# Layer 3's attention: score tiles on seven single PSUM banks, and six of a block's 32 row sums by accumulating DMA

## The chip, the cores and the metric

The kernel runs on one core of one Trainium2 chip. A core has TensorE (matrix products, written PE in the profile, its weight loads PEld), ScalarE (ACT: exponentials, copies with a scale), VectorE (DVE: elementwise work and reductions), GpSimd (POOL) and SyncE (SP), which run side by side and wait for each other by semaphores, and 16 DMA engines. SBUF is the working memory of 128 partitions. TensorE writes its results to PSUM, which has eight banks of 512 fp32 columns.

The metric is the device time of one execution in microseconds. Before the change it is 2603.03 us, the median of three runs from 2602.6 to 2603.3. The profiled execution has a span of 2601.4 us.

## The reference

The input is four images of 64 x 64 positions with 64 channels in fp32. Four layers run one after the other: a self-attention, a convolution block with layer norms, an attention of the data with itself, and a non-local block. Only the last one, called layer 3, is touched:

```python
N = H * W                                   # 4096 positions
g_x = (x @ g_W + g_b).reshape(B, N, 32)
phi_x = (x @ phi_W + phi_b).reshape(B, N, 32)
theta_x = (x @ theta_W + theta_b).reshape(B, N, 32)
f = einsum('bnd,bmd->bnm', theta_x, phi_x)
f = softmax(f, axis=-1)
y = einsum('bnm,bmd->bnd', f, g_x)
w_y = y @ w_W + w_b
...                                         # batch norm over all images
return x + w_y
```

For each image it makes a 4096 x 4096 matrix of scores, takes exponentials, multiplies them by `g_x`, and divides each row by its sum of exponentials. There are four images, so some 67 million exponentials in this layer.

## The kernel before, in words

**Order of the work.** One Python loop (`run`) lays out every engine's instructions by hand, as a list of items with work that is due some items later. The instruction streams keep that order. Layers 0 and 1 come first, for all images. Then layer 2 and layer 3 alternate: layer 2 of image 0, layer 2 of image 1, layer 3 of image 0, layer 2 of image 2, layer 3 of image 1, layer 2 of image 3, layer 3 of image 2, layer 3 of image 3. So the layer 3 stages of images 0 and 1 stand alone between layer 2 stages, and those of images 2 and 3 run directly one after the other.

**An item of layer 3.** An image's stage has 64 items, in two blocks (`nb`) of 32 (`mc`). A block is half of the image's rows, 2048 of them, as four groups of 512. An item pairs them with 128 of the 4096 columns. Its parts are:

- `scores(n)`, line 1419: eight small matmuls (32 deep, 64 wide, 512 columns) that fill four PSUM banks, all at once on different parts of the array. In the records each fp32 matmul stands twice, so an item has 16.
- two exponentials, lines 1424 and 1425, of 1024 columns each, from PSUM to a tile `e` of 128 x 2048 in SBUF. There are six such tiles in turn.
- `products(n)`, line 1454, issued two items later: four matmuls of `e` with `gx`, which accumulate over the block into one bank (`st["y"]`).
- the sum of exponentials over the columns. Most items add `e` to a running tile `esum` on VectorE (lines 1445 and 1447). Items 9, 19 and 29 of a block, and the last four of the last image, are summed by TensorE instead: four matmuls with a matrix of ones (line 1440) into a second accumulating bank, `st["z"]`.

**End of a block.** `sums` (line 1466) adds the total of `esum` to `st["z"]` by four more matmuls with ones. In the order of TensorE this stands after the scores of the fourth item of what follows, or two items later where layer 2 follows (images 0 and 1). ScalarE copies `st["y"]` out (L1460), takes the reciprocal of the sums as a logarithm and an exponential (L1474, L1477), VectorE refines it by a Newton step (L1482 to L1484), TensorE projects (L1501), ScalarE adds the bias (L1514) and VectorE takes statistics (L1516). In a block that follows directly, the second exponential of item 1 is held back until after the copy of `st["y"]`.

**PSUM.** `PS` is all eight banks. `new_ps` hands out slots of two banks (1024 columns); in layers 2 and 3 three slots take turns, which are banks 0 to 5. `new_acc` alternates between banks 6 and 7, for accumulators. A slot can be written by TensorE again only when ScalarE has read it.

**The `xn` tile.** One tile of 128 x 2048 in SBUF, used in layer 1 alone before the change.

Of the kernel before, what the change touches and what calls it, by code (L numbers as in the profile page):

```python
# [8 lines left out]
F32 = mybir.dt.float32  # L9
AF = mybir.ActivationFunctionType  # L10
ALU = mybir.AluOpType
# [680 lines left out]
def fast_path(ctx: ExitStack, tc: tile.TileContext, a: dict, out: bass.AP, bad):  # L692
    nc = tc.nc
# [10 lines left out]
    xn = ctx.enter_context(tc.tile_pool(name="xn", bufs=1))  # L704
# [4 lines left out]

    PS = pp.tile([128, 4096], F32, name="PS")
    turn_of = {"slots": [0, 1, 2, 3], "ps": 0, "acc": 0}

    def new_ps():
        s = turn_of["slots"][turn_of["ps"] % len(turn_of["slots"])]
        turn_of["ps"] += 1
        return PS[:, bass.ts(s, 1024)]

    def take_slots(*slots):  # L720
        turn_of["slots"], turn_of["ps"] = list(slots), 0

    def new_acc():
        turn_of["acc"] += 1
        return PS[:, bass.ts(6 + turn_of["acc"] % 2, 512)]

# [13 lines left out]
    act = nc.scalar.activation  # L740
# [9 lines left out]
    def fetch_x(b, queues):  # L750
# [17 lines left out]
        out=gam0, in_=a["L0_conv_gamma"].rearrange("(o n) -> o n", o=1).to_broadcast([128, 1])  # L768
# [94 lines left out]
    ones = const.tile([128, 64], F32, name="ones")  # L863
# [422 lines left out]
    def layer2(b):  # L1286
        x, m, first = X[:, b], im[b], len(items)
        xw = x.rearrange("p (w h) -> p w h", h=H)
        m.ph = None
        m.zs = sm.tile([128, 32, 4], F32, tag="zs2", name="zs2")  # L1290
        es, acc = {}, {}
        quads = ((0, 0), (1, 0), (0, 1), (1, 1))

        def scores(n):
            ib = n // 8
            for jb in range(4 * (n % 8), 4 * (n % 8) + 4):
                ps = new_ps()
                for r, c in quads:
                    rows_ = slice(64 * r, 64 * r + 64)
                    mm(  # L1300
                        ps[64 * c : 64 * c + 64, bass.ts(r, 512)],
                        m.ko[rows_, 128 * jb + 64 * c : 128 * jb + 64 * c + 64],
                        m.ko[rows_, bass.ts(2 * ib + r, 512)], start=True, stop=True,
                    )
                if jb % 2 == 0:
                    e = new_e()
                es[n, jb] = e[:, bass.ts(jb % 2, 1024)]
                act(es[n, jb], ps, AF.Exp, bias=SHIFT2, accum_out=m.zs[:, jb, ib : ib + 1])  # L1308
                follow(0)

        def products(n):
            ib = n // 8
            if n % 8 == 0:
                acc[0], acc[1] = new_acc(), new_acc()
            for jb in range(4 * (n % 8), 4 * (n % 8) + 4):
                for r, c in quads:
                    rows_ = slice(64 * r, 64 * r + 64)
                    mm(  # L1318
                        acc[r][64 * c : 64 * c + 64, :], xw[rows_, jb, :],
                        es[n, jb][rows_, bass.ts(c, 512)], start=jb == 0, stop=jb == 31,  # L1320
                    )
            if n % 8 == 7:
                if m.ph is None:
                    m.ph = new_big("ph")
                nc.scalar.copy(m.ph[:, 2048:2560], acc[0])  # L1325
                nc.vector.tensor_add(m.ph[:, 2048:2560], m.ph[:, 2048:2560], acc[1])  # L1326

        def turn(ib):
            ps = new_ps()
            for i in range(4):  # L1330
                nc.tensor.transpose(
                    ps[:, bass.ts(i, 128)], m.ph[:, 2048 + 128 * i : 2176 + 128 * i], ident
                )
# [23 lines left out]


    wys, early = {}, []
    small = {}  # L1360
    held = []

# [44 lines left out]
    def layer3(b):  # L1407
# [3 lines left out]
        def scores(n):  # L1411
            nb, mc = n // 32, n % 32
            e = es[n] = new_e()
            tiles = [new_ps(), new_ps()]
            for kp in range(2):
                for c in range(2):
                    for i in range(2):
                        rows_ = slice(64 * kp + 32 * i, 64 * kp + 32 * i + 32)
                        mm(  # L1419
                            tiles[kp][64 * c : 64 * c + 64, bass.ts(i, 512)],  # L1420
                            m.ph[rows_, 128 * mc + 64 * c : 128 * mc + 64 * c + 64],
                            m.th[rows_, bass.ts(nb, 512)], start=True, stop=True,
                        )
            act(e[:, 0:1024], tiles[0], AF.Exp)  # L1424
            held.append(lambda: act(e[:, 1024:2048], tiles[1], AF.Exp))  # L1425
            if not (mc == 1 and (nb or last)):
                held.pop()()
            for fn in small.get(first + n, []):
                fn()

        def products(n):
            nb, mc = n // 32, n % 32
            e, esum = es[n], m.tg[:, 2048:4096]
            if mc == 0:
                st["y"] = new_acc()
            if mc % 10 == 9 or (last and n >= 60):
                if mc == 9:
                    st["z"] = new_acc()
                for k in range(4):
                    mm(  # L1440
                        st["z"][32 * k : 32 * k + 32, :], ones[:, 0:32], e[:, bass.ts(k, 512)],
                        start=mc == 9, stop=False,
                    )
            elif mc == 1:
                nc.vector.tensor_add(esum, es[n - 1], e)
            elif mc:
                nc.vector.tensor_add(esum, esum, e)  # L1447
            if last and n == 62:
                return
            if last and n == 63:  # L1450
                sums()
            for i in (n - 1, n) if last and n == 63 else (n,):
                for k in range(4):
                    mm(  # L1454
                        st["y"][32 * k : 32 * k + 32, :], m.gx[:, i % 32, :], es[i][:, bass.ts(k, 512)],
                        start=mc == 0, stop=i % 32 == 31,
                    )
            if mc == 31 and not (last and n == 63):
                st["yz"] = new_t("yz")
                nc.scalar.copy(st["yz"][:, 0:512], st["y"])  # L1460
                if held:
                    held.pop()()

        def sums():
            for k in range(4):
                mm(
                    st["z"][32 * k : 32 * k + 32, :], ones[:, 0:32],
                    m.tg[:, 2048 + 512 * k : 2560 + 512 * k], start=False, stop=True,
                )


        def log(cols):
            st["inv"] = st.get("inv") or new_t("inv")
            act(st["inv"][:, cols], st["z"][:, cols], AF.Ln)  # L1474

        def exp(cols):
            act(st["inv"][:, cols], st["inv"][:, cols], AF.Exp, scale=-1.0)  # L1477

        def newton(nb):
            yz, z, t = st["yz"], st["z"], st.pop("inv")  # L1480
            r, d = t[:, 0:512], t[:, 512:1024]
            nc.vector.tensor_mul(d, z, r)  # L1482
            stt(d, d, -2.0, r, ALU.add, ALU.mult, accum_out=inv3[:, 2 * b + nb : 2 * b + nb + 1])
            stt(yz[:, 0:512], d, -1.0, yz[:, 0:512], ALU.mult, ALU.mult)  # L1484

        def totals(n):
            sums()
            steps = [
                lambda: log(slice(0, 256)), lambda: log(slice(256, 512)),
                lambda: exp(slice(0, 256)), lambda: exp(slice(256, 512)), lambda: newton(n // 32),  # L1490
            ]
            for i, fn in enumerate(steps):
                if n == 63 and b < 2:
                    fn()
                else:
                    small.setdefault(first + n + 5 + min(i, 3), []).append(fn)
# [296 lines left out]
```

## Time and profile before

| | us | of the span |
|---|---|---|
| span of the profiled execution | 2601.4 | |
| TensorE busy | 2572.4 | 99% |
| ScalarE busy | 1770.1 | 68% |
| VectorE busy | 1162.7 | 45% |
| GpSimd busy | 14.3 | 1% |
| layer 3, image 0: item 3's scores to item 63's | 134.0 | |
| layer 3, image 1: the same | 134.0 | |
| layer 3, images 2 and 3: item 3's scores to the last item's | 287.1 | |
| VectorE's adds of `e` (L1447), 213 of 2.291 us | 488.0 | |
| exponentials of layer 3 (L1424, L1425), 512 | 524.2 | |
| sums on TensorE (L1440), 216 records | 28.5 | |

Times are microseconds. "Busy" is the time in which an engine executes at least one instruction; TensorE's matmuls are pipelined, several at once on different parts of the array, and their ends are modelled, so that its busy share tells little. The start times are better evidence. A group in the profile is a line of the kernel, an engine and an operation, with the tile written, an arrow, and the tiles read; a busy time and a mean in nanoseconds of one; and after a bar the idle time of the engine before it, with what ended that idle time.

### The profile page before, as it was taken

What the parts mean: (1) busy time and instruction counts of PE and PEld (TensorE: products, weight loads), DVE (VectorE), ACT (ScalarE), POOL (GpSimd) and SP (SyncE); (2) the same over time, 40 slices, a digit from 0 to 9 for tenths busy, and PEclk for the clock granted to TensorE, in tenths of its full rate; (3) what the DMA queues carried; (4) which work ended last, traced back from release to release, by engine and by line L of the source; (5) the groups of instructions that cost most, each with busy time, mean ns of one, the idle gap of its engine ahead of it and who ended that gap; (6) DMA issues with size and microseconds to landing.
All of it is one profiled execution on the core that took longest, in us unless ns stands there. A gap on an engine that the chain in (4) does not pass through costs nothing.

```text
span 2601.4 us, 55343 instructions
## 1 busy us (share of the span) xinstructions
PE 2572.4 (99%) x24477; PEld 870.8 (33%) x24477; DVE 1162.7 (45%) x1302; ACT 1770.1 (68%) x2814; POOL 14.3 (1%) x46
## 2 busy tenths in 40 slices
PE   9999999999999999999999999999999999999998
PEld 3343333333333345333333322233322333322223
DVE  2010266312672237613671168610078500098996
ACT  4666766667666676666656578756588655678886
POOL 2000000000000000000000000000000000000000
PEclk9999999999999999999999999999999999999999
DMA  3000000001000000010010000010000010010002
GB/s 75 1 18 1 17 18 2 17 2 34 1 2 17 17 17 2 1 33 18 1 34 17 18 1 2 2 34 1 18 1 2 4 31 1 1 34 2 1 2 67
DMA packets 24557, 36.75 MB, mean 14 GB/s; under 512 B 3724, under 2 KB 12149, under 8 KB 24309
## 3 DMA queue, kind: packets, MB, share of 16 engines
q1 hardware_dynamic: 22853, 30.72, 5.3%
q8 instruction: 194, 3.18, 0.5%
q10 hardware_dynamic: 752, 1.85, 0.2%
q0 software_dynamic: 704, 0.56, 0.1%
q14 instruction: 54, 0.44, 0.1%
HBM read 4.80 MB, written 4.19 MB: 3 GB/s over the span
## 4 chain that ended last, share of the span: by engine, by line
PE 96%; ACT 2%; DVE 1%; issue 0%; DMA 0%; SPq 0%; ACTq 0%; DVEq 0%
PE PS L1318 17%; PE PS L1300 17%; PE PS L1095 16%; PE PS L1069 16%; PE PS L1419 11%; PE PS L1454 10%; PE PS L1179 2%; PE PS L1440 1%; ACT e L1074 1%; PE PS L1037 1%; PE PS L1241 1%; PE PS L1264 1%; PE PS L1144 1%; PE PS L1398 1%; ACT q L1019 0%; PE PS L952 0%
## 5 line engine op out<-in xcount | busy, mean ns | idle before, releaser
L1074 ACT ACTIVATE e<-PS 128x1024 f32<-128x1024 f32 x512 | 524.1, 1024 | 326.8 <-PE PS L1069 284.2
L1308 ACT ACTIVATE e<-PS 128x1024 f32<-128x1024 f32 x512 | 517.2, 1025 | 292.3 <-PE PS L1300 289.1
L1095 PE MATMUL PS<-e,vq 64*64 64x512 f32 x4096 | 539.9, 591 | 0.0
L1069 PE MATMUL PS<-X,q 64*64 64x512 f32 x4096 | 537.1, 590 | 1.8 <-DVE X L953 1.7
L1447 DVE TENSOR_TENSOR tg<-tg,e 128x2048 f32<-128x2048 f32 x213 | 488.0, 2291 | 23.9 <-ACT e L1425 5.7
L1300 PE MATMUL PS<-ko 64*64 64x512 f32 x4096 | 469.2, 591 | 2.2 <-ACT ko L1282 1.7
L1318 PE MATMUL PS<-e,X 64*64 64x512 f32 x4096 | 464.1, 591 | 0.0
L1424 ACT ACTIVATE e<-PS 128x1024 f32<-128x1024 f32 x256 | 262.8, 1027 | 84.4 <-PE PS L1419 63.6
L1212 DVE SCALAR_TENSOR_TENSOR y<-pad,vec,y 128x1024 f32<-128x1024 f32 x240 | 308.1, 1284 | 8.2 <-ACT pad L1196 1.1
L1419 PE MATMUL PS<-tg,ph 32*64 32x512 f32 x4096 | 311.0, 613 | 0.5 <-ACT e L1424 0.5
L1454 PE MATMUL PS<-e,tg 128*32 128x512 f32 x2048 | 271.8, 603 | 0.0
L1425 ACT ACTIVATE e<-PS 128x1024 f32<-128x1024 f32 x256 | 261.4, 1021 | 0.0
L1069 PEld LDWEIGHTS PS<-X,q 64*64 64x64 f32 x4096 | 161.2, 133 | 279.3 <-issue 231.9
L1300 PEld LDWEIGHTS PS<-ko 64*64 64x64 f32 x4096 | 156.5, 132 | 290.1 <-issue 199.8
L1095 PEld LDWEIGHTS PS<-e,vq 64*64 64x64 f32 x4096 | 160.7, 133 | 272.8 <-issue 171.3
L1318 PEld LDWEIGHTS PS<-e,X 64*64 64x64 f32 x4096 | 155.5, 133 | 275.0 <-issue 271.6
L1082 DVE TENSOR_REDUCE sums<-zs 128x1 f32<-128x4 f32 x128 | 19.9, 155 | 374.3 <-ACT e L1074 374.2
L1326 DVE TENSOR_TENSOR ph<-ph,PS 128x512 f32<-128x512 f32 x16 | 11.0, 687 | 391.7 <-ACT ph L1325 391.7
L1419 PEld LDWEIGHTS PS<-tg,ph 32*64 32x64 f32 x4096 | 80.6, 129 | 217.2 <-issue 119.7
L1454 PEld LDWEIGHTS PS<-e,tg 128*32 128x32 f32 x2048 | 43.6, 108 | 201.0 <-issue 196.9
L1308 ACT ACTIVATION_READ_ACCUMULATOR e<-PS 128x1 f32 x512 | 106.5, 208 | 0.0
L1074 ACT ACTIVATION_READ_ACCUMULATOR e<-PS 128x1 f32 x512 | 99.6, 194 | 0.1
(193 smaller groups left out, 947.5 us busy)
## 6 DMA issues: line engine op xcount, KB each, us to landing
xn<-t SPq DMA_DIRECT2D x64, 128.0 KB
ph<-tg SPq DMA_DIRECT2D x64, 128.0 KB
ko<-ko SPq DMA_DIRECT2D x16, 256.0 KB
xr<-in_x_dram SPq DMA_DIRECT2D x13, 256.0 KB
q<-q SPq DMA_DIRECT2D x12, 256.0 KB
out_dram<-o SPq DMA_DIRECT2D x7, 256.0 KB
out_dram<-o ACTq DMA_DIRECT2D x2, 512.0 KB
out_dram<-o SPq DMA_DIRECT2D x2, 512.0 KB
```

The source lines that it names most:

```text
L1069: mm(ps[64 * c : 64 * c + 64, bass.ts(r, 512)], m.q[rows_, 128 * t + 64 * c : 128 * t + 64 * c + 64], x[rows_, bass.ts(g, 512)], start=Tru ...
L1074: act(es[g // 2][:, bass.ts(g % 2, 1024)], ps, AF.Exp, bias=SHIFT0, accum_out=zs[:, g : g + 1],)
L1095: ins = mm(PS[64 * s : 64 * s + 64, 2048 + 512 * j : 2560 + 512 * j], vq[rows_, :], es[j // 2][rows_, k : k + 512], start=t == 0 and i < 2 ...
L1212: stt(y1, win, wt, y1, ALU.mult, ALU.add)
L1300: mm(ps[64 * c : 64 * c + 64, bass.ts(r, 512)], m.ko[rows_, 128 * jb + 64 * c : 128 * jb + 64 * c + 64], m.ko[rows_, bass.ts(2 * ib + r, 5 ...
L1308: act(es[n, jb], ps, AF.Exp, bias=SHIFT2, accum_out=m.zs[:, jb, ib : ib + 1])
L1318: mm(acc[r][64 * c : 64 * c + 64, :], xw[rows_, jb, :], es[n, jb][rows_, bass.ts(c, 512)], start=jb == 0, stop=jb == 31,)
L1419: mm(tiles[kp][64 * c : 64 * c + 64, bass.ts(i, 512)], m.ph[rows_, 128 * mc + 64 * c : 128 * mc + 64 * c + 64], m.th[rows_, bass.ts(nb, 51 ...
L1424: act(e[:, 0:1024], tiles[0], AF.Exp)
L1425: held.append(lambda: act(e[:, 1024:2048], tiles[1], AF.Exp))
L1447: nc.vector.tensor_add(esum, esum, e)
L1454: mm(st["y"][32 * k : 32 * k + 32, :], m.gx[:, i % 32, :], es[i][:, bass.ts(k, 512)], start=mc == 0, stop=i % 32 == 31,)
```

## The change

It has three parts, all in layer 3.

- **Single banks in turn.** `take_banks(7)` makes `new_bank` hand out banks 0 to 6 one by one. An item takes four, and the next item goes on where it stopped. Bank 7 is `st["y"]` for all blocks. `st["z"]` is no longer an accumulator over the block: `totals` takes one bank from the turn for the closing sums, VectorE copies it into `yz` and so frees it. For the last two items of the last image the turn is restarted on six banks, since bank 6 is then `st["z"]`. Layer 2 goes back to three slots with `take_slots`.
- **First exponential on one bank.** An item's exponentials are one of 512 columns and one of 1536, in place of two of 1024. Where the three banks of the latter wrap from 6 to 0, it is cut in two.
- **Six sums by DMA, none on TensorE.** The `e` tiles of items 3, 7, 11, 15, 19 and 23 of each block go into the `xn` tile by DMA from GpSimd's queue, in two halves of 1024 columns each: the first is a plain copy, the other five accumulate. At item 27 VectorE adds that tile to `esum`. TensorE's sums at items 9, 19 and 29 are gone; those of the last image's last four items stay.

The aim is to let TensorE start an item's scores without waiting for ScalarE, and to take the sums off it without giving VectorE more to do.

```diff
+    def new_bank():
+        if not turn_of["banks"]:
+            turn_of["ps"] += 1
+            return 2 * turn_of["slots"][(turn_of["ps"] - 1) % len(turn_of["slots"])]
+        turn_of["bank"] += 1
+        return (turn_of["bank"] - 1) % turn_of["banks"]
...
+    BY_DMA = (3, 7, 11, 15, 19, 23)
...
-            tiles = [new_ps(), new_ps()]
+            if n == 0 and (b < 3 or not turn_of["banks"]):
+                take_banks(7)
+            if last and n == 62:
+                take_banks(6)
+            banks = [new_bank() for _ in range(4)]
...
-            act(e[:, 0:1024], tiles[0], AF.Exp)
-            held.append(lambda: act(e[:, 1024:2048], tiles[1], AF.Exp))
-            if not (mc == 1 and (nb or last)):
-                held.pop()()
+            def exp(lo, hi):
+                while lo < hi:
+                    k = lo + 1
+                    while k < hi and banks[k] == banks[k - 1] + 1:
+                        k += 1
+                    act(
+                        e[:, 512 * lo : 512 * k],
+                        PS[:, 512 * banks[lo] : 512 * banks[lo] + 512 * (k - lo)], AF.Exp,
+                    )
+                    lo = k
+
+            exp(0, 1)
+            if mc == 1 and (nb or last):
+                held.append(lambda: exp(1, 4))
+            else:
+                exp(1, 4)
+            if mc in BY_DMA:
+                if mc == BY_DMA[0]:
+                    st["dma"] = xn.tile([128, 2048], F32, tag="xn", name="xn")
+                for h in range(2):
+                    cols = bass.ts(h, 1024)
+                    if mc == BY_DMA[0]:
+                        nc.gpsimd.dma_start(out=st["dma"][:, cols], in_=e[:, cols])
+                    else:
+                        nc.gpsimd.dma_start(out=st["dma"][:, cols], in_=e[:, cols], accum_op=ALU.add)
...
-            if mc % 10 == 9 or (last and n >= 60):
-                if mc == 9:
-                    st["z"] = new_acc()
+            st["y"] = PS[:, 3584:4096]
+            if last and n >= 60:
+                st["z"] = PS[:, 3072:3584]
...
-            elif mc:
+            elif mc and mc not in BY_DMA:
                 nc.vector.tensor_add(esum, esum, e)
+            if mc == BY_DMA[-1] + 4:
+                nc.vector.tensor_add(esum, esum, st["dma"])
...
         def totals(n):
-            sums()
+            k = new_bank()
+            z = PS[:, bass.ts(k, 512)]
+            sums(z, True)
+            nc.vector.tensor_copy(st["yz"][:, 512:1024], z)
```

More of the change, by code (lines that the diff above doesn't have):

```diff
@@ L712, in fast_path, with take_banks @@
     PS = pp.tile([128, 4096], F32, name="PS")
-    turn_of = {"slots": [0, 1, 2, 3], "ps": 0, "acc": 0}
-    def new_ps():
+    turn_of = {"slots": [0, 1, 2, 3], "ps": 0, "acc": 0, "banks": 0, "bank": 0}
+    def new_bank():
[4 more added lines that the diff above has]
+        return (turn_of["bank"] - 1) % turn_of["banks"]
+    def take_banks(n):
+        turn_of["banks"], turn_of["bank"] = n, 0
+    def new_ps():
+        if turn_of["banks"]:
+            if turn_of["bank"] % turn_of["banks"] == turn_of["banks"] - 1:
+                turn_of["bank"] += 1
+            k = new_bank(), new_bank()
+            return PS[:, 512 * k[0] : 512 * k[0] + 1024]
         s = turn_of["slots"][turn_of["ps"] % len(turn_of["slots"])]
@@ L720, in take_slots @@
     def take_slots(*slots):
-        turn_of["slots"], turn_of["ps"] = list(slots), 0
+        turn_of["slots"], turn_of["ps"], turn_of["banks"] = list(slots), 0, 0
     def new_acc():
@@ L1295, in scores @@
             ib = n // 8
+            if n == 0 and b:
+                take_slots(0, 1, 2)
             for jb in range(4 * (n % 8), 4 * (n % 8) + 4):
@@ L1417, in scores @@
                     for i in range(2):
-                        rows_ = slice(64 * kp + 32 * i, 64 * kp + 32 * i + 32)
+                        k = 2 * kp + i
                         mm(
-                            tiles[kp][64 * c : 64 * c + 64, bass.ts(i, 512)],
-                            m.ph[rows_, 128 * mc + 64 * c : 128 * mc + 64 * c + 64],
-                            m.th[rows_, bass.ts(nb, 512)], start=True, stop=True,
-                        )
-            act(e[:, 0:1024], tiles[0], AF.Exp)
-            held.append(lambda: act(e[:, 1024:2048], tiles[1], AF.Exp))
-            if not (mc == 1 and (nb or last)):
-                held.pop()()
+                            PS[64 * c : 64 * c + 64, bass.ts(banks[k], 512)],
+                            m.ph[32 * k : 32 * k + 32, 128 * mc + 64 * c : 128 * mc + 64 * c + 64],
+                            m.th[32 * k : 32 * k + 32, bass.ts(nb, 512)], start=True, stop=True,
+                        )
+            def exp(lo, hi):
[22 more added lines that the diff above has]
+                        nc.gpsimd.dma_start(out=st["dma"][:, cols], in_=e[:, cols], accum_op=ALU.add)
             for fn in small.get(first + n, []):
@@ L1433, in products @@
             e, esum = es[n], m.tg[:, 2048:4096]
-            if mc == 0:
-                st["y"] = new_acc()
-            if mc % 10 == 9 or (last and n >= 60):
-                if mc == 9:
-                    st["z"] = new_acc()
+            st["y"] = PS[:, 3584:4096]
+            if last and n >= 60:
+                st["z"] = PS[:, 3072:3584]
                 for k in range(4):
@@ L1441, in products @@
                         st["z"][32 * k : 32 * k + 32, :], ones[:, 0:32], e[:, bass.ts(k, 512)],
-                        start=mc == 9, stop=False,
+                        start=n == 60, stop=False,
                     )
@@ L1450, in products @@
             if last and n == 63:
-                sums()
+                sums(st["z"], False)
             for i in (n - 1, n) if last and n == 63 else (n,):
@@ L1462, in products, with sums @@
                     held.pop()()
-        def sums():
+        def sums(z, alone):
             for k in range(4):
                 mm(
-                    st["z"][32 * k : 32 * k + 32, :], ones[:, 0:32],
-                    m.tg[:, 2048 + 512 * k : 2560 + 512 * k], start=False, stop=True,
+                    z[32 * k : 32 * k + 32, :], ones[:, 0:32],
+                    m.tg[:, 2048 + 512 * k : 2560 + 512 * k], start=alone, stop=True,
                 )
@@ L1473, in log @@
             st["inv"] = st.get("inv") or new_t("inv")
-            act(st["inv"][:, cols], st["z"][:, cols], AF.Ln)
+            act(st["inv"][:, cols], st["yz"][:, 512 + cols.start : 512 + cols.stop], AF.Ln)
         def exp(cols):
@@ L1479, in newton @@
         def newton(nb):
-            yz, z, t = st["yz"], st["z"], st.pop("inv")
+            yz, t = st["yz"], st.pop("inv")
             r, d = t[:, 0:512], t[:, 512:1024]
-            nc.vector.tensor_mul(d, z, r)
+            nc.vector.tensor_mul(d, yz[:, 512:1024], r)
             stt(d, d, -2.0, r, ALU.add, ALU.mult, accum_out=inv3[:, 2 * b + nb : 2 * b + nb + 1])
@@ L1486, in totals @@
         def totals(n):
-            sums()
+            k = new_bank()
+            z = PS[:, bass.ts(k, 512)]
+            sums(z, True)
+            nc.vector.tensor_copy(st["yz"][:, 512:1024], z)
             steps = [
```

## Prediction

> **What bounds the kernel now.** I read the page first, for the engines' shares and the costliest groups, and then only layer 3, since nothing else is changed.
>
> ```profile
> PE 2572.4 (99%) x24477; PEld 870.8 (33%) x24477; DVE 1162.7 (45%) x1302; ACT 1770.1 (68%) x2814; POOL 14.3 (1%) x46
> ...
> L1447 DVE TENSOR_TENSOR tg<-tg,e 128x2048 f32<-128x2048 f32 x213 | 488.0, 2291 | 23.9 <-ACT e L1425 5.7
> ...
> L1424 ACT ACTIVATE e<-PS 128x1024 f32<-128x1024 f32 x256 | 262.8, 1027 | 84.4 <-PE PS L1419 63.6
> L1419 PE MATMUL PS<-tg,ph 32*64 32x512 f32 x4096 | 311.0, 613 | 0.5 <-ACT e L1424 0.5
> ```
>
> The page calls TensorE 99% busy, but its matmuls are pipelined and a group that starts late still counts as busy. So I looked at TensorE's start times inside layer 3, in the timeline (start, length, engine, line).
>
> ```profile
> 1558.63 1.22 PE L1419 MATMUL PS<-tg,ph 32*64 32x512 f32 x16
> 1559.77 1.06 PE L1440 MATMUL PS<-e,ones 128*32 128x512 f32 x8
> 1560.66 1.04 PE L1454 MATMUL PS<-e,tg 128*32 128x512 f32 x8
> 1561.63 1.11 PE L1419 MATMUL PS<-tg,ph 32*64 32x512 f32 x16
> 1562.67 1.06 PE L1454 MATMUL PS<-e,tg 128*32 128x512 f32 x8
> 1563.67 1.28 PE L1419 MATMUL PS<-tg,ph 32*64 32x512 f32 x16
> 1564.88 1.06 PE L1454 MATMUL PS<-e,tg 128*32 128x512 f32 x8
> 1565.87 1.11 PE L1419 MATMUL PS<-tg,ph 32*64 32x512 f32 x16
> ```
>
> An item is scores (L1419) and products (L1454). The one at 1561.63 lasts 1.04 + 1.00 = 2.04 us; the next 1.21 + 0.99 = 2.20. The 0.17 more is scores waiting for a PSUM slot that ScalarE still reads. The sum wave at 1559.77 adds 0.89, of which its neighbour gives back 0.03: 0.86. So an item costs TensorE 2.04 us, waits apart, and a sum on TensorE 0.86.
>
> VectorE is nearly as full there. Its timeline at a block's end, and the stage's windows (span, PE, PEld, DVE, ACT busy):
>
> ```profile
> 1581.73 4.69 DVE L1447 TENSOR_TENSOR tg<-tg,e 128x2048 f32<-128x2048 f32 x2 [0.31 <-ACT e L1425]
> 1592.78 2.29 DVE L1445 TENSOR_TENSOR tg<-e 128x2048 f32<-128x2048 f32 x1 [6.36 <-PE PS L1466]
> 1595.17 7.08 DVE L1447 TENSOR_TENSOR tg<-tg,e 128x2048 f32<-128x2048 f32 x3
> 1603.25 0.69 DVE L1482 TENSOR_TENSOR inv<-PS,inv 128x512 f32<-128x512 f32 x1 [0.99 <-ACT inv L1477]
> ```
> ```profile
> 1519.50:1653.50 134.00, 134.00 (x1500) 30.16 (x1496) 119.48 (x58) 117.72 (x126) 0.00 (x0) 1.00 0.01 1
> ...
> 2276.60:2563.70 287.10, 287.10 (x3192) 67.45 (x3188) 263.95 (x141) 247.05 (x267) 0.00 (x0) 1.00 0.04 9
> ```
>
> From 1592.78 to 1595.17 an add takes 2.39 us with the gap behind it: more than TensorE's 2.04 for the item. VectorE keeps pace now only because TensorE sums every tenth item and items take 2.12 with their waits. The first window runs from item 3's scores to item 63's: 60 items x 2.04 + 7 sum waves x 0.86 + one projection 1.02 = 129.4, so about 4.6 of 134 are waits.
>
> **The skill.** "DMA: Bandwidth & Descriptors", section "SWDGE vs HWDGE vs iDMA": an accumulating DMA can be issued from GpSimd alone, which writes its descriptors. That engine is free: 14.3 us busy in all, at about 0.5 us per DMA issue in its timeline. The same page, "Anatomy of one DMA": some 2 us of fixed cost and then bytes at 436 GB/s. The trace shows less, on copies to 64 partitions: in slices of 0.15 us the copies into ko moved 297 GB/s at best, and a 2.6 us window of the copies into q 202. "Collectives: The Full Stack", section "The bandwidth ceiling": a reducing DMA reads two sources for each write and reached half the rate of a copy. No run here shows an accumulating DMA. "SBUF — State Buffer", section "Who interferes with whom": a VectorE add of two SBUF operands contends with GpSimd's reads, not with descriptor writes. I lean on that; this trace has no GpSimd work beside such adds.
>
> **Sums taken off TensorE.** Line 1440 had three sums in each of seven blocks and six in the last, 27 in all (216 matmul records, 8 each); the new kernel keeps the last block's four. 23 x 0.86 = 19.8 us leave TensorE's path. The closing sums of each block (L1466, 0.86) stay.
>
> **Seven single banks.** Before, an item took two 1024-column slots of three, so the next item's first quad reused the slot of the item before last and its second that of the last item's first exponential. Scores end 1.04 us after they start, the first exponential starts 0.1 later and lasts 1.02: free at 2.17, wanted at 2.04. Hence the waits. Adding L1419's distance to the next group over all 256 items gives 294.0 us, against 256 x 1.044 = 267.3: 26.7 us of waits, some 20 in the steady state. Now only the item's last bank needs the former item's first exponential, of 512 columns. By the 512-column copy (L1325, 587 ns) it ends at 1.15 + 0.59 = 1.74, before 2.04. ScalarE's work barely grows: 1024-column exponentials follow each other at 0.92, that is 0.427 for 512 columns and 0.067 for an instruction. An item needs 4 x 0.427 + 2 x 0.067 = 1.84, and two items in seven, whose last three banks wrap, one instruction more: 1.86 on average. Under 2.04, so hidden, but with only 0.18 to recover from the copy (0.59), logs and exponentials (0.4 each) and output activation (1.12) of a block. I leave 1 us of waits for a block, 8 in all.
>
> **VectorE.** It does 25 adds and one for the DMA's tile, instead of 28. That is 26 x 2.39 = 62.1, a new copy of the sums of about 0.65, Newton steps 2.1, two statistics 1.3: 66.2 us for a block. Round trips are idle time on top: sums to copy about 1.5, reciprocals to Newton 1 to 2. About 69. TensorE wants 32 x 2.04 + 0.86 + 1.02 = 67.2. VectorE therefore becomes the bound, late in the block: from item 24 there are nine adds in a row. Exponentials of item 24 are done about 3.1 us after its scores start; nine adds take 21.6, so the last ends 24.7 after that, while TensorE reaches the closing sums at 11 items + 1.04 = 23.5. It waits 1.2 us after a first block. The next block starts about 5 us late on VectorE, adds 3.5 of Newton and statistics, wins back 1 us in each group of four (8.16 against 3 x 2.39 = 7.17) and so carries about 2 us on: waits of about 2.9 after each later block, but only 1.3 in layer 3's end for images 0 and 1, where two layer 2 items come before the sums.
>
> **DMA.** A DMA'd item is 1.05 MB in two halves. Bounds: 3.5 us (297 GB/s, no penalty for accumulating) and 10.4 (202 GB/s, halved). I take 7, double the 3.5, since these copies span all 128 partitions. The next comes after four items, 8.16 us, and e is reused six items later: its exponentials end at 3.1 us and the new one may start at 12.24 + 1.15, which leaves 10.3 for issue (0.6), 7 and the 2 of the fixed cost: 9.6. Hidden, by 0.7 us. The GpSimd queue holds nothing else.
>
> **The sum.** A two-block layer (images 0, 1), item 3 to item 63: 122.4 + 0.86 + 1.02 + 1.2 + 1 = 126.5 against 134.0; with 1.3 at its end, 6.2 won, twice: 12.4. The four blocks of images 2 and 3, item 3 to item 127: 124 x 2.04 = 253.0, three closings of 1.88 = 5.6, two sums kept 1.7, waits 1.2 + 2.9 + 2.9, banks 2: 269.3 against 287.1: 17.8 won. Entering and leaving the stages I take as even: shorter waits in the first items, about 1 us lost where the last two items restart on six banks. 2603 - 30 = 2573 us.
>
> **Rivals.** All waits go: VectorE catches up, 19.8 + 26.7 minus some 4 at stage starts: 2560. For it: VectorE had slack of 6.36 at 1592.78. Against: that slack exists because TensorE came late, and it is the time I remove. Half the gain: DMA takes 9 us, or ScalarE's small margin makes banks wait. At 9, each of four intervals in a block slips 0.84 and the hold is over by 1.3: 4.7 x 8 = 37, less 14 of VectorE's waits that then vanish: 2596. Slower: the accumulate runs at the slow end, 10 us: 4 x 1.84 + 2.3 = 9.7 for a block, 78 in all, less 14: 2637. Exponentials then wait for e, and scores behind them. For it: copies at 202 GB/s in this trace, and the halving. Against: those reach half of the partitions, and the last eight items of a block have no DMA, which drains a backlog.
>
> **How the numbers follow.** Forecast 0.62; all waits gone 0.09; half 0.11; slower 0.18. The predicted time is the forecast's, 2573. The range starts at 2560; its upper end, 2604, takes in the half case and leaves the slow one out. Faster: 0.62 + 0.09 + most of the half case, 0.79; within 0.2% 0.03; slower 0.18.
>
> **What would show it.** The scores' distance to products should be 1.04 almost everywhere; VectorE over 95% busy in layer 3, idle in groups of four early in a block; TensorE waiting for VectorE at the closing sums by 1 to 3 us. A DMA'd half should be done within 10 us of its exponential. If first exponentials wait for DMA at items 9, 13 and so on, the slow case is there. Longer VectorE adds beside the GpSimd issues, or an issue well over 1 us, would break the sum.

## The result, and the profile after

The changed kernel takes 2574.29 us (median of four runs, 2573.77 to 2579.38), the one before 2602.84 beside it: a ratio of 0.9894, 95% interval 0.9877 to 0.9912. That is 28.6 us less. The forecast was 2573, in a range of 2560 to 2604.

The page after, first the engines' shares and then the groups of layer 3 (line numbers are those of the changed kernel: 1442 scores, 1453 exponentials, 1490 adds).

```profile
PE 2535.7 (99%) x24293; PEld 847.4 (33%) x24293; DVE 1129.0 (44%) x1292; ACT 1774.2 (69%) x2888; POOL 93.5 (4%) x142
...
L1453 ACT ACTIVATE e<-PS 128x512 f32<-128x512 f32 (+2 forms) x586 | 501.4, 923 | 48.3 <-PE PS L1442 28.1
...
L1490 DVE TENSOR_TENSOR tg<-tg,e 128x2048 f32<-128x2048 f32 x188 | 430.8, 2292 | 32.9 <-ACT e L1453 17.8
L1442 PE MATMUL PS<-tg,ph 32*64 32x512 f32 x4096 | 293.7, 613 | 0.2
```

ScalarE's exponentials cost a little more than before: 501.4 us against 496.2, both counted as the time in which at least one of them runs. (The 524.2 of the table before adds the busy times of two lines, and so counts the overlap of neighbours twice.) They are 586 instructions and not 512, since 74 are cut at the wrap. VectorE does 25 adds of `e` fewer in L1490, and eight of the DMA's tile come in (L1492). The 56 adds that run beside one of GpSimd's DMA issues take 2.290 us on average and the others 2.292, so these issues do not slow them. GpSimd is busy 93.5 us, not 14.3, in DMA issues.

TensorE's timeline inside a block of image 0:

```profile
1560.95 1.11 PE L1442 MATMUL PS<-tg,ph 32*64 32x512 f32 x16
1562.00 1.06 PE L1499 MATMUL PS<-e,tg 128*32 128x512 f32 x8
1562.99 1.11 PE L1442 MATMUL PS<-tg,ph 32*64 32x512 f32 x16
1564.04 1.06 PE L1499 MATMUL PS<-e,tg 128*32 128x512 f32 x8
1565.03 1.11 PE L1442 MATMUL PS<-tg,ph 32*64 32x512 f32 x16
```

From one item's scores to the next it is 2.04 us each time: the alternation of 2.04 and 2.20 is gone, and no sum wave stands between items.

Adding the distance from each TensorE group's start to the next group's start, over both traces from the first matmul of layer 2 on, tells where the time went (the groups that differ by more than 0.2 us):

| groups on TensorE | before, us | after, us | difference |
|---|---|---|---|
| sums in items (L1440; L1483) | 23.8 | 3.5 | -20.3 |
| scores of layer 3 (L1419; L1442) | 294.0 | 281.9 | -12.1 |
| products of layer 3 (L1454; L1499) | 253.7 | 257.1 | +3.4 |
| scores of layer 2 (L1300; L1318) | 450.2 | 451.6 | +1.5 |
| turning of layer 2's output (L1331; L1349) | 10.1 | 9.4 | -0.7 |

They sum to -28.2; the span of the profiled run is 29.4 less, since that run also began these stages 1.1 us earlier (995.7 us after its start, not 996.8; the other profiled runs lie between 995.3 and 996.8).

Two waits are new. At a block's closing sums TensorE waits for VectorE's last add, here in image 0:

```profile
1583.48 1.57 PE L1442 MATMUL PS<-tg,ph 32*64 32x512 f32 x16
1585.60 1.06 PE L1511 MATMUL PS<-tg,ones 128*32 128x512 f32 x8 [0.55 <-DVE tg L1490]
```

The scores begin at 1583.48 and the sums at 1585.60, 2.12 later and not 1.04. A part of that lies in the scores themselves, which last 1.57 us and not 1.11; run 7 below tells whose it is. And where layer 3 of images 0 and 1 gives way to layer 2, that layer's first scores wait for the last item's exponentials, and some scores later TensorE waits for ScalarE again:

```profile
1644.92 1.07 PE L1499 MATMUL PS<-e,tg 128*32 128x512 f32 x8
1647.07 3.66 PE L1318 MATMUL PS<-ko 64*64 64x512 f32 x32 [1.08 <-ACT e L1453]
...
1660.42 1.09 PE L1318 MATMUL PS<-ko 64*64 64x512 f32 x8 [0.51 <-ACT e L1326]
```

Layer 2 takes banks 0 and 1 first, and the last item of layer 3 sits on banks 5, 6, 0 and 1. This costs 1.15 us, and the later wait 0.75, each twice.

VectorE in image 3, across a block's end:

```profile
2405.61 0.69 DVE L1535 COPY yz<-PS 128x512 f32<-128x512 f32 x1 [1.34 <-PE PS L1511]
2406.22 2.28 DVE L1488 TENSOR_TENSOR tg<-e 128x2048 f32<-128x2048 f32 x1
2408.61 4.69 DVE L1490 TENSOR_TENSOR tg<-tg,e 128x2048 f32<-128x2048 f32 x2
2416.14 0.69 DVE L1527 TENSOR_TENSOR inv<-yz,inv 128x512 f32<-128x512 f32 x1 [2.85 <-ACT inv L1522]
...
2423.97 38.09 DVE L1490 TENSOR_TENSOR tg<-tg,e 128x2048 f32<-128x2048 f32 x16
2462.09 2.29 DVE L1492 TENSOR_TENSOR tg<-tg,xn 128x2048 f32<-128x2048 f32 x1
```

It stands still for 1.34 us (for the sums) and 2.85 (for the reciprocals), and for the rest of the block it adds without a break. The copies of the sums at two neighbouring block ends are 69.7 us apart: there the closing sums hang on VectorE's last add.

The DMA, in a window of 10 us that holds the first accumulating item of image 0 (share of the 16 engines in tenths, and GB/s, in slices of 0.25 us):

```profile
DMA  0000000075999989969994999769910000000009
GB/s 0 0 0 0 0 0 0 0 147 98 279 246 197 180 164 262 180 115 229 262 213 82 229 262 262 147 131 246 262 17 16 0 0 0 0 0 0 0 0 262
```

The engines are busy for 5.8 us, mostly at nine tenths, and then idle until the next item.

### The profile page after: what moved, and what is told of

The parts are those of the page before. It is cut to its first block, busy times and chain, and to the rows that moved or that the text cites. A ratio compares the mean times of both kernels' runs of the same rounds, so it can differ in the third digit from the quotient of the medians.

```text
span 2572.0 us, 55249 instructions
## 1 busy us (share of the span) xinstructions
PE 2535.7 (99%) x24293; PEld 847.4 (33%) x24293; DVE 1129.0 (44%) x1292; ACT 1774.2 (69%) x2888; POOL 93.5 (4%) x142
## 4 chain that ended last, share of the span: by engine, by line
PE 90%; DVE 4%; ACT 4%; issue 1%; DMA 0%; DVEq 0%; SPq 0%; ACTq 0%
PE PS L1336 17%; PE PS L1318 17%; PE PS L1111 17%; PE PS L1085 16%; PE PS L1442 8%; PE PS L1499 7%; DVE tg L1490 3%; PE PS L1195 2%; ACT e L1453 2%; ACT e L1090 1%; PE PS L1053 1%; PE PS L1257 1%; PE PS L1280 1%; PE PS L1160 1%; PE PS L1417 1%
## 5 line engine op out<-in xcount | busy, mean ns | idle before, releaser
L1090 ACT ACTIVATE e<-PS 128x1024 f32<-128x1024 f32 x512 | 523.7, 1023 | 326.1 <-PE PS L1085 283.8
L1326 ACT ACTIVATE e<-PS 128x1024 f32<-128x1024 f32 x512 | 516.7, 1024 | 292.8 <-PE PS L1318 289.6
L1453 ACT ACTIVATE e<-PS 128x512 f32<-128x512 f32 (+2 forms) x586 | 501.4, 923 | 48.3 <-PE PS L1442 28.1
L1318 PE MATMUL PS<-ko 64*64 64x512 f32 x4096 | 469.7, 591 | 5.4 <-ACT e L1453 2.2
L1490 DVE TENSOR_TENSOR tg<-tg,e 128x2048 f32<-128x2048 f32 x188 | 430.8, 2292 | 32.9 <-ACT e L1453 17.8
L1442 PE MATMUL PS<-tg,ph 32*64 32x512 f32 x4096 | 293.7, 613 | 0.2
L1499 PE MATMUL PS<-e,tg 128*32 128x512 f32 x2048 | 272.4, 604 | 0.0
L1318 PEld LDWEIGHTS PS<-ko 64*64 64x64 f32 x4096 | 156.5, 132 | 293.9 <-issue 200.3
L1442 PEld LDWEIGHTS PS<-tg,ph 32*64 32x64 f32 x4096 | 62.9, 129 | 217.5 <-ACT e L1453 185.1
L1499 PEld LDWEIGHTS PS<-e,tg 128*32 128x32 f32 x2048 | 41.4, 108 | 205.6 <-issue 201.6
L1470 POOL DMA_DIRECT2D xn<-e x16 | 8.8, 559 | 2139.2 <-PE PS L1442 1504.3
```

What stands on the lines that cost most here:

```text
L1090: act(es[g // 2][:, bass.ts(g % 2, 1024)], ps, AF.Exp, bias=SHIFT0, accum_out=zs[:, g : g + 1],)
L1318: mm(ps[64 * c : 64 * c + 64, bass.ts(r, 512)], m.ko[rows_, 128 * jb + 64 * c : 128 * jb + 64 * c + 64], m.ko[rows_, bass.ts(2 * ib + r, 5 ...
L1442: mm(PS[64 * c : 64 * c + 64, bass.ts(banks[k], 512)], m.ph[32 * k : 32 * k + 32, 128 * mc + 64 * c : 128 * mc + 64 * c + 64], m.th[32 * k ...
L1453: act(e[:, 512 * lo : 512 * k], PS[:, 512 * banks[lo] : 512 * banks[lo] + 512 * (k - lo)], AF.Exp,)
L1499: mm(st["y"][32 * k : 32 * k + 32, :], m.gx[:, i % 32, :], es[i][:, bass.ts(k, 512)], start=mc == 0, stop=i % 32 == 31,)
```

## The experiments

The sums of the last image's last four items stay on TensorE in all of them. Each ratio is to the kernel before, run on the same chip; its medians lie between 2602.63 and 2603.03 us, so that times of different experiments can be set beside each other to about half a microsecond, apart from each run's own range.

**1. The sums alone.** The kernel before with the DMA sums of the new one and its old slots (the main lines of the edit):

```diff
-            if mc % 10 == 9 or (last and n >= 60):
+            if last and n >= 60:
...
-            elif mc:
+            elif mc and mc not in BY_DMA:
                 nc.vector.tensor_add(esum, esum, e)
+            if mc == BY_DMA[-1] + 4:
+                nc.vector.tensor_add(esum, esum, st["dma"])
```

> The kernel before with only the sums changed: six items of a block by DMA, none on TensorE, and the old three slots of two banks and two exponentials of 1024 columns. My theory: the 23 sum waves go (19.8 us), the 26.7 us of waits for a PSUM slot stay: about 2583 us. Rival one, the waits were only a by-product of the sum waves or of VectorE: 2575 or less. Rival two, the banks carry the gain and the sums are worth little, since VectorE or the DMA takes their place: 2595 or more.

Measured: 2584.68 us (2584.02 to 2585.34), ratio 0.993, interval 0.9916 to 0.9944; 18.0 us less than before. Scores of layer 3 sum to 296.3 us, that is 29.0 of waits where the kernel before has 26.7. So the sum waves were worth nearly their own time, the waits for PSUM do not hang on them, and the rest, 10.4 us, is the banks' part.

**2. Seven banks with exponentials of two and two.**

```diff
-            exp(0, 1)
+            exp(0, 2)
...
-                exp(1, 4)
+                exp(2, 4)
```

> The changed kernel with seven banks, but each item's exponentials split two banks and two in place of one and three. My theory: the next item's last bank then waits for an exponential of 1024 columns, free at 2.17 us where it is wanted at 2.04, so some 0.1 us for an item come back, less what VectorE's waits at the closing sums give up: 2588 to 2595. Rival, that seven banks alone remove the waits: 2574 to 2577.

Measured: 2585.14 us (2583.95 to 2585.45), ratio 0.993, interval 0.9917 to 0.9944. It is a little faster than expected, and 10.9 us slower than the changed kernel: all of the banks' part. TensorE's timeline shows the old alternation again:

```profile
1560.97 1.11 PE L1442 MATMUL PS<-tg,ph 32*64 32x512 f32 x16
...
1563.01 1.27 PE L1442 MATMUL PS<-tg,ph 32*64 32x512 f32 x16
...
1565.21 1.11 PE L1442 MATMUL PS<-tg,ph 32*64 32x512 f32 x16
```

2.04 and 2.20 us. Seven banks alone remove nothing; with the short first exponential they do.

**3. One DMA in place of six.**

```diff
-            if mc in BY_DMA:
+            if mc == BY_DMA[0]:
```

> The changed kernel with the first DMA of a block alone, the five accumulating ones left out, so that five items of 32 are missing from the row sums; VectorE's work is the same. My theory, the DMA is hidden: 2573 to 2575. Rival, the DMA holds the e tiles, or GpSimd's issues slow VectorE's adds: faster by 5 us or more, 2569 or less.

Measured: 2574.04 us (2573.47 to 2575.96), ratio 0.9889, interval 0.9873 to 0.9904: no different from the changed kernel, with the same waits at the closing sums. The five accumulating DMAs of a block are hidden, but for one wait of 0.7 us that ScalarE has in the changed kernel's image 2.

**4. Closing sums two items later.**

```diff
-                    small.setdefault(first + n + 5 + min(i, 3), []).append(fn)
+                    small.setdefault(first + n + 7 + min(i, 3), []).append(fn)
...
-                at(first + n + (2 if n == 63 and b < 2 else 4), lambda n=n: totals(n))
-                at(first + n + 11, lambda n=n: close(n // 32))
+                at(first + n + (2 if n == 63 and b < 2 else 6), lambda n=n: totals(n))
+                at(first + n + 13, lambda n=n: close(n // 32))
```

> The changed kernel with the closing sums of a block that is followed by layer 3 items, and what follows from them, two items later in TensorE's order. My theory: TensorE's waits for VectorE there, 1.1 us three times and about 2.2 twice, 7.6 in all, shrink: 2568 to 2570. Rival, VectorE is the bound over the whole stage, and the time comes back at the next block's end: 2573 to 2575.

Measured: 2574.88 us (2574.78 to 2575.51), ratio 0.9893, interval 0.9878 to 0.9909. The edit does more than I meant: in that place the next block's first adds have been written over `esum` already, so that the sums are those of the next block's first two adds, and TensorE waited for these instead. It says nothing on the theory; runs 5 and 7 take it up again.

**5. Eight DMA items, every third.**

```diff
-    BY_DMA = (3, 7, 11, 15, 19, 23)
+    BY_DMA = (2, 5, 8, 11, 14, 17, 20, 23)
```

> The changed kernel with eight items of a block by DMA, every third from 2 to 23, in place of six. VectorE has two adds (4.8 us) less in each block. My theory has two causes for TensorE's waits at the closing sums: nine adds in a row at a block's end (1.1 us in each of the five closings inside layer 3), and work carried over from the block before (1.1 us more in the last two). Eight DMA items take away the second alone: 2571 to 2573. Rival: a DMA item every 6.1 us is too much for the DMA, e tiles are held, 2580 or more.

Measured: 2577.25 us (2576.04 to 2579.73), ratio 0.9905, interval 0.9889 to 0.9922. The time lies between the theory's and the rival's. At the closing sums it went nearly as expected: 1.08 and 1.07 us in images 0 and 1, 0.79 in image 2, and 1.07 and 1.14 in image 3 where the changed kernel has 2.24 and 2.13. But from image 1's last closing sums to the first of image 2 TensorE takes 309.5 us and not 305.8. There the scores of two items take 2.6 and 0.9 us longer, and ScalarE waits 3.0 for a DMA of e. This is where image 3's `ph` tile is filled by DMAs from SyncE's queue.

**6. Six banks.**

```diff
-                take_banks(7)
+                take_banks(6)
```

> The changed kernel with six single banks in turn in place of seven, all else the same. My theory: two of three items then need a bank that the former item's second exponential, of three banks, is still reading: free at 3.1 us where it is wanted at 2.04, about 0.7 us for an item on average, 150 to 190 us in all: 2725 to 2765. Rival, that the split of the exponentials matters and not the seventh bank: 2574 to 2600.

Measured: 2701.72 us (2701.33 to 2702.41), ratio 1.0381, interval 1.0364 to 1.0398. 127 us lost, less than the 150 to 190 expected: in TensorE's timeline three items in turn lose 1.06, 0.60 and nothing, 0.55 on average and not 0.7. The seventh bank and the split need each other.

**7. DMA items later.**

```diff
-    BY_DMA = (3, 7, 11, 15, 19, 23)
+    BY_DMA = (7, 11, 15, 19, 23, 27)
```

> The changed kernel with its six DMA items at 7, 11, 15, 19, 23 and 27 of a block in place of 3 to 23; the DMA's tile is then added at item 31. VectorE's work is the same, but the adds in a row at a block's end are five and not nine. My theory: the 1.1 us at each of the five closing sums go, and what is carried over stays: 2569 to 2571. Rival, that VectorE's whole work in a block sets the waits, so that only their place changes: 2573 to 2575.

Measured: 2570.86 us (2570.55 to 2572.22), ratio 0.9879, interval 0.9863 to 0.9896. The time is as expected, but not for the reason given. Each of the five closings now costs 0.79 us, as 0.45 and 0.34 us in the scores of two items in images 0 and 1 and at the first of image 3, and in one piece at the other two. The wait is for ScalarE and no longer for VectorE, as in image 3:

```profile
2466.75 2.29 DVE L1492 TENSOR_TENSOR tg<-tg,xn 128x2048 f32<-128x2048 f32 x1
2470.26 1.07 PE L1511 MATMUL PS<-tg,ones 128*32 128x512 f32 x8 [0.26 <-ACT e L1453]
```

VectorE's last add ends at 2469.04, 1.2 us before the sums start; at the other four closings it is 0.8 to 1.3 us early. So both waits for VectorE went, that of the row of adds and the carried one, and what is left is ScalarE's, which had lain under them: the first three closings fell by 0.3 us and the last two by 1.4. VectorE does as many adds in a block as in the changed kernel. So the rival fails too: it was the place of these adds that TensorE waited for, and not their number alone. VectorE's timeline in image 3 has one add more ahead of the Newton steps, and less idle time there:

```profile
2405.79 7.08 DVE L1490 TENSOR_TENSOR tg<-tg,e 128x2048 f32<-128x2048 f32 x3
2413.62 0.69 DVE L1527 TENSOR_TENSOR inv<-yz,inv 128x512 f32<-128x512 f32 x1 [0.75 <-ACT inv L1522]
```

**8. Eight DMA items, later.** `BY_DMA = (6, 9, 12, 15, 18, 21, 24, 27)`.

> Both at once: eight items of a block by DMA, every third from 6 to 27, the DMA's tile added at item 31. My theory: all of TensorE's waits for VectorE at the closing sums go, 7.6 us: 2566 to 2568. Rival, DMA too slow at one item in 6.1 us: 2580 or more.

Measured: 2576.96 us (2573.99 to 2578.14), ratio 0.9898, interval 0.9881 to 0.9914. In images 0 and 1 its layer 3 is that of run 7 to 0.1 us: one DMA item in 6.1 us fits. In image 2 it loses 7.5 us against run 7 (313.2 and 305.7 from image 1's last closing sums to image 2's first), and ScalarE's timeline shows by what (the profiled run is one of the slower of the four, 2577.88 us):

```profile
2327.40 2.49 ACT L1453 ACTIVATE e<-PS 128x512 f32<-128x512 f32 x4 [4.84 <-DMA xn<-e]
```

From 2310 us on the 16 engines are 9 tenths full for some 12 us, at about 190 GB/s and with both queues' transfers, and an e half lands a median 7.9 us after its issue. So the DMA was hidden, but with little room: the rival of a slow DMA came true for one image once its rate was raised by a third.

**9. Leaving layer 3.** Run 7 with:

```diff
-                take_slots(0, 1, 2)
+                take_slots(*((1, 2, 0) if turn_of["banks"] else (0, 1, 2)))
...
-            k = new_bank()
+            k = 6 if n == 63 and b < 2 else new_bank()
```

> The kernel with the DMA items at 7 to 27, and two edits where layer 3 gives way to layer 2 (images 0 and 1): layer 2 takes its slots in the order 1, 2, 0, since the last item's exponentials still read banks 0 and 1; and the last sums use bank 6 in place of a slot. In the changed kernel's timeline TensorE waits there 1.15 and 0.75 us, twice. My theory: 3.8 us less than with the DMA items moved alone: 2566 to 2568. Rival, that ScalarE is behind there and the wait only moves on to layer 2's next items: 2570 to 2571.

Measured: 2568.49 us (2567.47 to 2569.5), ratio 0.9866, interval 0.9851 to 0.9881, the fastest version of these, 5.8 us below the changed kernel. The first wait is gone (products 1645.47, layer 2's scores 1646.47). The second stayed at 0.68 us, so that the bank of the last sums is not its cause. So the theory holds for 2.3 of 3.8 us, the rival for the rest. Why ScalarE is behind there stands in the traces, in the changed kernel and in the one before:

```profile
1656.81 0.60 ACT L1505 COPY yz<-PS 128x512 f32<-128x512 f32 x1
1658.04 0.72 ACT L1519 ACTIVATE inv<-yz 128x256 f32<-128x256 f32 x2 [0.62 <-DVE yz L1535]
```
```profile
1666.28 0.60 ACT L1460 COPY yz<-PS 128x512 f32<-128x512 f32 x1
1666.75 0.70 ACT L1474 ACTIVATE inv<-PS 128x256 f32<-128x256 f32 x2
```

Before, the logarithms read the sums from PSUM and followed ScalarE's copy at once. Now they read VectorE's new copy of the sums, and ScalarE stands still for 0.62 us (0.55 in run 9) until it is there, with layer 2's exponentials behind it. The change itself brought in this round trip; no run takes it out.

**10. No DMA.** Items 9, 19 and 29 are left out of the row sums, and VectorE adds 28 items.

```diff
-            if mc in BY_DMA:
+            if False:
...
-            elif mc and mc not in BY_DMA:
+            elif mc and mc % 10 != 9:
...
-            if mc == BY_DMA[-1] + 4:
+            if False:
```

> The changed kernel without any DMA of e: VectorE adds all items but 0, 9, 19 and 29, 28 adds in a block as in the kernel before, and those three are left out of the row sums altogether. TensorE's work is that of the changed kernel. My theory: VectorE then needs some 73 us for a block against TensorE's 67, and TensorE waits for it at the closing sums or ScalarE for e tiles: 2600 to 2615, all of the gain gone. Rival, that VectorE has slack enough and the DMA is not needed: 2574 to 2580.

Measured: 2585.82 us (2584.95 to 2587.82), ratio 0.9937, interval 0.9924 to 0.9951. The direction is the theory's, the size is not: 11.5 us, not 26 to 41. At the end of a first block 28 adds still fit: the closings in images 0, 1 and 2 cost the 0.79 us that are ScalarE's. In image 3 TensorE waits 3.5 us at each of the two closings, whose distance grows from 69.7 to 74.1. The DMA is worth 11.5 us, in blocks that follow another.

**11. DMA items one later.** `BY_DMA = (4, 8, 12, 16, 20, 24)`.

> The changed kernel with the DMA items one later, at 4, 8, 12, 16, 20 and 24. Eight adds in a row stand at a block's end in place of nine, and item 3 is an add, which VectorE can do while it would otherwise wait 2.9 us for the reciprocals of the block before. My theory, formed on the run with the DMA items at 7 to 27: that idle time is what carried work over into the next block, and with it filled TensorE's waits at the last two closing sums fall from 2.2 us to the 0.8 of eight adds, as the other three do: 2570 to 2572. Rival, that only the length of the row of adds matters: each of the five falls by 0.3 us alone, 2573 or more.

Measured: 2574.01 us (2572.56 to 2575.59), ratio 0.9887, interval 0.987 to 0.9903. I had miscounted: item 3 is now an add, but item 4 is none, and both stand ahead of the Newton steps. VectorE's idle time stayed at 2.85, and the last two waits at 2.15 and 2.09. The shorter row of adds took 0.3 us off the waits in images 0 and 1, as expected of its length, but almost nothing in image 2 (1.05) and image 3. The time does not tell the two apart; the trace says that neither expectation was whole.

**12. Newton steps later.**

```diff
-                    small.setdefault(first + n + 5 + min(i, 3), []).append(fn)
+                    small.setdefault(first + n + 5 + (i if i < 3 else 3 if i == 3 else 5), []).append(fn)
...
-                at(first + n + 11, lambda n=n: close(n // 32))
+                at(first + n + 12, lambda n=n: close(n // 32))
```

> The changed kernel with VectorE's Newton steps two items later in its order, and the projection one item later; the DMA items are at 3 to 23 as in the changed kernel. In the run with the DMA items one later, VectorE's idle time of 2.9 us ahead of the Newton steps had stayed, since as many adds stood ahead of them, and so had TensorE's waits of 2.1 us at the last two closing sums. My theory: two more adds ahead of the Newton steps fill that idle time; the first three waits stay at 1.1, the last two fall from 2.2 to about 1.1: 2571 to 2573. Rival, that the idle time does not matter to the block: all five waits stay, 2574.

Measured: 2573.97 us (2573.01 to 2575.71), ratio 0.9891, interval 0.9874 to 0.9907. The idle time ahead of the Newton steps is gone, and a new one of 2.46 stands ahead of the statistics, which wait for ScalarE's output:

```profile
2417.85 0.68 DVE L1527 TENSOR_TENSOR inv<-yz,inv 128x512 f32<-128x512 f32 x1
...
2424.65 1.29 DVE L1564 BATCH_NORM_STATS2 bst<-wy 128x6 f32<-128x512 f32 x2 [2.46 <-ACT wy L1562]
```

The block stays at 69.4 and 69.8, and the last two closings wait 2.0 and 2.4 us. So idle time was moved, not removed, and the theory that it makes the carry is neither shown nor refuted by this run. In run 7 the carry went, but there the row of adds at a block's end was shorter and the idle time ahead of the Newton steps too; no run separates the two.

## Why the prediction was right, point by point

**Sum waves: right.** 19.8 us; the table has 20.3, of which neighbouring products give back 0.5. Alone they brought 18.0 (run 1).

**Banks: right in mechanism.** The step that the first exponential of one bank frees it at 1.74 us, before 2.04, is what runs 2 and 6 test; in the trace it ends 1.73 to 1.79 us after its item's scores start, and items at 2.04 us follow. Of waits 14.6 us are left in the scores, where there were 26.7: 7.6 at the closings, 3.9 at the stages' first items, 1.1 at the restart on six banks (predicted 1), and 2.0 for all else. The text of the prediction leaves 8 us for ScalarE's recovery, but its sum takes in only 4.

**VectorE: the waits are there, but its work is not the bound.** TensorE does wait for VectorE at the closing sums. The waits were forecast as 1.2 us in a first block, 2.9 in a later one and 1.3 at the end of images 0 and 1; they are 1.1, 2.2 and none, in all 7.6 and not 12.0. "About 69" us for a block is 69.7, though its idle time is 4.2 and not 2.5 to 3.5. The prediction took this to mean that VectorE's work bounds the block. Run 7, with the same work in another order, has no closing that waits for VectorE. So a first block's wait comes from the nine adds that stand late in it, which the prediction names as well; what carries more of it into later blocks is not settled (run 12). The sign "over 95% busy" is not there either. In these windows (span, then PE, PEld, DVE and ACT busy) VectorE has 88% in image 0 and just over 90% in images 2 and 3:

```profile
1518.11:1643.87 125.76, 125.14 (x1460) 24.32 (x1456) 110.46 (x55) 119.04 (x144) 19.80 (x24) 1.00 0.49 102
2260.10:2534.22 274.12, 269.94 (x3100) 56.09 (x3097) 248.09 (x136) 249.24 (x301) 39.59 (x48) 1.00 0.49 101
```

And 0.79 us of each closing is ScalarE's, as run 7 shows, so that VectorE adds only 3.7 of the 7.6. The forecast put ScalarE's waits and VectorE's one after the other; at the closings they overlap.

**DMA: right.** The copy of 1.05 MB, the first of a block, took 2.85 us in five of the eight blocks and 3.8 to 5.0 in the others, for which no run shows the cause. The accumulating one took 5.35 to 6.98, against the 7 I chose between 3.5 and 10.4. From the first issue to the last landing an accumulating item takes 7.1 to 8.8 us, where I had 9.6 of 10.3; two items of image 2 beside SyncE's copies take 9.4 and 10.5. The 4 KB packets took 159 and 339 ns: a factor 2.1. That is near the half rate that the Trainium skill's "Collectives: The Full Stack", section "The bandwidth ceiling: the fold count and why AG ≠ RS ≠ AR", puts down to two source reads for each write. That the reads are the reason here as well, no run shows. Run 3 shows the DMA hidden. GpSimd's issue takes a median 0.88 us where a plain copy's takes 0.56, and up to 1.23. The prediction named an issue well over 1 us as a sign against it; it did no harm, since GpSimd does nothing else then and VectorE's adds got no longer.

**Errors that cancelled.** Of the 30 us forecast, 32.8 were to be won between item 3 and the last item of the stages, and 2.6 lost after them; the traces have 29.5 and 1.1. The four-block sum, 269.3 us, is now 274.1. I had left out image 3's preparation (three projections), which lies inside image 2's stage: from item 3 to item 63 that stage takes 140.6 us before and image 0's 134.0. So 6.6 of the 17.8 us won there did not exist. The window won 12.9, and not the 11.2 that remain, since its waits at the closings were smaller and only one of the two sums kept lies inside it. On the other side images 0 and 1 won 8.3 each between items 3 and 63, where I had 7.5, and lost nothing at the closing sums after it. And "entering and leaving the stages I take as even" was wrong: leaving costs 3.8 us (run 9 takes 2.3 of it back), against 1.8 won by two sum waves that fell just behind the window. The total of 30 met the measured 28.6 partly by luck. One more slip has no part in the sum: the first window before holds six sum waves (five in items and a closing one) and not seven, so that 5.4 of its 134 us were waits and not 4.6.

**Rivals.** "All waits go" (2560) failed. A part of the reason given is borne out: VectorE's slack was TensorE's lateness, for in run 10, with as many adds as before and no sum waves, TensorE waits 3.5 us at two closings. But VectorE is not the whole reason. In run 7 no closing waits for it, and the time is still 2570.9: 11.0 us of waits are left in the scores, most of them at the stages' first items and for ScalarE at the closings. The slow DMA did not come about at one item in 8.16 us; at one in 6.1 it did, in image 2 (runs 5 and 8).

## What to carry to other kernels

Where two engines hand buffers to each other in turn, ask when each buffer is released and when it is wanted, and not only how many there are: seven banks with a short first instruction removed the wait, seven with even halves did not, and six with uneven ones cost 127 us against the kernel with seven. When work is taken off the bounding engine, walk the next one's queue through a whole block, with its rows of work and its round trips. A sum of its work doesn't tell whether it holds the other up: the same adds cost 3.4 us less when they no longer stood in a row at the block's end (run 7). And put every other piece of work that lies inside a window into both sides of a sum before reading a gain from it.

## What the runs showed of the hardware that I had not expected

A plain copy of 1.05 MB over all 128 partitions ran at 368 GB/s (2.85 us) in five of eight blocks. Copies to 64 partitions in the kernel before had shown 202 in mean (into `q`), and 297 in the best slice of those into `ko`. They were DMAs of 256 KB in packets of 2 KB or less, where the new ones have 512 KB in packets of 4 KB, so that these runs don't tell whether the partitions or the sizes made the difference. An accumulating DMA in SBUF ran at 150 to 196 GB/s, and slower only beside SyncE's copies in image 2.
